# Passing from the per-pixel convolution to the spline convolution: where the first tiles lie, and in which order they are loaded

## The chip, the cores and the metric

The kernel runs on one core of a Trainium2 chip. The core has five engines that work from queues of their own: TensorE (PE in the profile), VectorE (DVE), ScalarE (ACT), GpSimd (POOL) and SyncE (SP). SP issues most transfers here. They are carried out by 16 DMA engines and end by raising a semaphore. The metric is the device time of one execution in microseconds (us), as the median of several runs. Beside it stands one profiled execution, from which all durations come.

## The reference

The input x has 4 images of 16 channels and 256x256 pixels. Two layers follow, each with a residual and with a group norm (8 groups of 2 channels) in front:

```python
x = x + _L0_conv_ref(_gn(x), conv_w, conv_b)
#   out = conv3x3(x): 16*25 numbers a pixel; weights = softmax over the 25
#   result = sum over the 5x5 neighbours of each channel, times weights
x = x + _L1_conv_ref(_gn(x), base_weight, spline_weight, spline_scaler, bias_weight)
#   patches = 3x3 neighbours
#   out = silu(patches) . base_w + B_splines(patches) . spl_w + bias
```

The B-splines are of order 3 on 8 bases: each value of x becomes 8 features, so 16 channels give 128 features, one for each partition of the on-chip memory. The 3x3 sum over them is a matrix product.

## The kernel before, in words

**Layer 0** works in 64 strips: 4 images, 2 halves of 128 rows, 8 strips of 32 columns. A row of the image is a partition. For each 4 columns of a strip, PE makes 400 logits for each pixel from the loaded tiles am and an (L922, L926), ACT takes exp into a tile e (L945), POOL multiplies e by the neighbours u (L950), and DVE sums both halves over the 25 taps into nd (L771). A few steps later each strip is finished: ACT makes the reciprocal's seed from nd (L785, L787), DVE divides and refines (L791, L795, L799), and POOL subtracts the quotient, which stands in nd, from the strip's x (L805). The sum x1 goes to a buffer in the device's memory, x1s. For the last strip of all, POOL issues the two stores itself (L862), behind its L805.

**Layer 1** works in 64 units of 16 image rows (16 units an image). A unit loads its rows of x1 twice: once as 128 features, each channel repeated 8 times (`load_x`, L1029, two transfers of 1 MB into one of three tiles xta, xtb, xtc), and once as plain rows for silu (`load_tiles`, L1041, four transfers of 128 KB into one of three buffers sl). ACT turns the features into distances from the spline's knots (`distance`, L1068), DVE and ACT make the inner part r1 (`inner`, L1077 and L1075), ACT squares it into s1 (`square`, L1082), POOL multiplies to the cube (`cube`, L1089; some squares too, L1085), ACT makes the outer part (`far`, L170), DVE multiplies it and combines both into a ring of rows (`cubed`, `combined`: L173, L176). ACT takes silu of the plain rows (L1051), and PE sums ring and silu over the 3x3 taps (`outputs`, L1229, L1238). Tiles of unit n are those of number n modulo 3 (xt, sl) or modulo 2 (s1).

**The passage.** Layer 1's instructions are placed between those of layer 0's end: while POOL and DVE finish the last strip, ACT already makes unit 0's distance, inner part and square. Each engine runs its queue strictly in order. `in_order` and `behind` fix the order on ACT, DVE, POOL and SP by hand. Three places matter here.

- `load_x(0)`, `load_tiles(0)`, `load_x(1)`, `load_x(2)`, `load_tiles(1)` (L1250 to L1254) set SP's order after layer 0's last loads.
- `start_unit` does unit 0's first steps. Then `first_features` begins with unit 1's distance, which needs xtb, and DVE's inner part of unit 1, which reads it, stands in DVE's queue after the first two chunks of unit 0.
- `for t in sl: sides(t)` (L1268, its memsets are L1257) lets POOL zero the edge columns of the three sl buffers, after the last strip's L805.

**Memory.** Layer 0's pools are given back before layer 1's are made, and layer 1's tiles are laid on the same addresses. `fixed` opens a pool with its tiles, one pool a call, in the order of the calls. The first instruction that touches such a pool's memory waits for the layer-0 instructions that still use it. Of layer 0, in order of address: norm's and transpose's tiles, then an and am (pool im), u and e (one pool, l0), nd, x1's strips xc. Layer 1 before, in order of address: xta, r1a, r1b, s1a, s1b, xtb, pad, ring, xtc, sl (three buffers in one pool), yo. There xtb begins on am and ends on u, xtc lies on e, and the sl pool begins on e and runs over nd.

Of the kernel before, what the change touches and what calls it, by code (L numbers as in the profile page):

```python
# [34 lines left out]
def conv_preact_kernel(  # L35
# [13 lines left out]
    B, C, H, W = x.shape  # L49
    G = 8  # L50
    GC = C // G
    P = 128
# [21 lines left out]
    RT = 2  # L74
    NT = P // (RT * C)
    RD = RT + 2
    RU = 16
# [897 lines left out]
    def layer1(arm, last, marks, seeds):  # L975
# [5 lines left out]
        with ExitStack() as pools:  # L981
            def pool(name, bufs=1, **kw):
                return pools.enter_context(tc.tile_pool(name=f"{name}{arm}", bufs=bufs, **kw))


            def fixed(name, shape, n=1):
                p = pool(name)
                t = [p.tile(shape, F32, name=f"{name}{k}{arm}") for k in range(n)]
                return t

            XT = [P, RU + 1, W]
# [1 line left out]
            SQ = 2 * QR + 2  # L993
            xt0 = fixed("xta", XT)
            r1a, r1b = fixed("r1a", [P, 3 * QR, W])[0], fixed("r1b", [P, QR + 1, W], 2)
            s1s = fixed("s1a", XT) + fixed("s1b", [P, RU, W])
            xt1, pad = fixed("xtb", XT), fixed("pad", [P, W + 2])[0]
            ring = fixed("ring", [P, 2 * RU + 2, W + 2])[0]
            SL = [P, RU // RT, W + 2]
            xtt = xt0 + xt1 + fixed("xtc", XT)  # L1000
            sl = fixed("sl", SL, 3)
            yop = pool("yo", 3)
            ps2 = pool("ps2", 2, space=PSUM)
            py = pool("py", 2, space=PSUM)
# [5 lines left out]
            def rows(t, dims, r):  # L1010

                return bass.AP(tensor=t.tensor, offset=t.offset + r * W, ap=dims)
# [4 lines left out]
            def cuts(u):  # L1017
                lo, hi = span(u)
                return [(a, min(a + QR, hi)) for a in range(lo, hi, QR)]
# [5 lines left out]
            def load_x(n):  # L1025
                b, u = units[n]
                c = cuts(u)
                for a, z in ((c[0][0], c[1][1]), (c[2][0], c[-1][1])):
                    nc.sync.dma_start(  # L1029
                        xs(n, a, z),  # L1030
                        rows(x1s[b], [[CP, 2 * C], [0, SH], [1, (z - a) * W]], u * RU + a),
                    )

            def xs(n, a, z):
                lo = span(units[n][1])[0]
                return xtt[n % 3][:, a - lo : z - lo, :]

            def load_tiles(n):
                b, u = units[n]
                for d in range(RD):  # L1040
                    nc.sync.dma_start(  # L1041
                        sl[n % 3][P // 2 + d : P : RD, :, 1 : W + 1],
                        rows(x1s[b], [[CP, C], [RT * W, RU // RT], [1, W]], u * RU + d),
                    )
# [203 lines left out]
                for b in range(2, B)  # L1248
            ))
            load_x(0)  # L1250
            load_tiles(0)
            load_x(1)
            load_x(2)
            load_tiles(1)  # L1254
            def sides(t):
# [50 lines left out]
    with tc.If(fast > 0) as small_logits:  # L1306
        layer1("", *layer0(False))
    with small_logits.Else():
        layer1("g", *layer0(True))
# [42 lines left out]
```

## Time and profile before

| | |
|---|---|
| median of 3 runs | 2956.73 us (2956.46 to 2959.94) |
| profiled execution, its time | 2963.85 us |
| its span, first to last instruction | 2962.1 us |
| busy: PE, DVE, ACT, POOL | 93%, 96%, 73%, 91% |
| mean granted PE clock | 0.969 of full speed |
| DMA | 647.60 MB, 219 GB/s on the mean |
| layer 0's last matmul begins | 2021.83 us from the span's start |

A row of a timeline has its start, its duration, the engine ("SPq" is the issue of a transfer by SP), the line of the kernel, the operation, the tiles written and read, and how often it was done. Brackets hold the idle time before it and what ended that by the profile. A row of stretches has, for each engine, busy time and number of instructions. A row of waits has who waited for whom, the total in us, how often, and the longest.

### The profile page before, as it was taken

The page shows a single profiled execution, that of the slowest core. Times are in us where ns is not written, and L with a number is a line of the kernel's source. Part 1 is how long each engine was busy: PE and PEld are TensorE (multiplying, and loading weights), DVE is VectorE, ACT ScalarE, POOL GpSimd, SP SyncE. Part 2 cuts the span into 40 slices and gives each one's busy share as a digit, 9 for nine tenths or more (in the row PEclk, how much of TensorE's full clock was granted, in tenths as well). Part 3 has the DMA queues.
Part 4 walks back from the last instruction along what each step waited for, and adds up shares of the span by engine and source line. Part 5 has one row for each costly group of instructions (what it writes and reads, how often), then busy time and mean ns, then how long its engine had stood idle before and what let it go on. Part 6 is the DMA issues. An engine that isn't in the chain of part 4 may idle for free.

```text
span 2962.1 us, 40885 instructions
## 1 busy us (share of the span) xinstructions
PE 2749.8 (93%) x14282; PEld 1490.7 (50%) x14282; DVE 2841.2 (96%) x1866; ACT 2161.9 (73%) x2764; POOL 2703.9 (91%) x1116
## 2 busy tenths in 40 slices
PE   4699999999999999999999989993999999999998
PEld 3466666666666566656656656662323323222222
DVE  7599999999999999999999999996999999999997
ACT  6566876667766567667565554565999999999995
POOL 4399999999999999999999999996898999999895
PEclk7799999999999999999999999996999999999999
DMA  9998999889888789899786766774577676777763
GB/s 276 250 240 230 253 262 249 237 219 253 238 235 231 214 218 239 218 246 243 211 218 173 197 180 173 197 195 155 182 228 221 209 238 208 225 221 223 224 213 102
DMA packets 385736, 647.60 MB, mean 219 GB/s; under 512 B 41842, under 2 KB 250180, under 8 KB 369652
## 3 DMA queue, kind: packets, MB, share of 16 engines
q1 hardware_dynamic: 321556, 609.73, 73.1%
q10 hardware_dynamic: 61920, 31.46, 3.9%
q0 software_dynamic: 2048, 3.72, 0.5%
q8 instruction: 117, 1.92, 0.3%
q14 instruction: 95, 0.78, 0.1%
HBM read 516.18 MB, written 121.15 MB: 215 GB/s over the span
## 4 chain that ended last, share of the span: by engine, by line
DVE 38%; PE 22%; ACT 22%; DMA 7%; issue 6%; SPq 2%; POOL 2%; ACTq 0%; DVEq 0%; POOLq 0%
DVE nd L771 31%; PE lg L922 14%; ACT s L170 4%; PE lg L926 4%; ACT sl L1051 3%; PE yp L1229 3%; ACT xtc L1068 3%; ACT xta L1068 2%; ACT xtb L1068 2%; ACT s1a L1082 2%; ACT s1b L1082 2%; ACT r1b L1075 2%; POOL e L950 2%; DMA am<-hst 2%; DMA an<-hsl 1%
## 5 line engine op out<-in xcount | busy, mean ns | idle before, releaser
L950 POOL TENSOR_TENSOR e<-e,u 128x1600 f32<-128x1600 f32 x512 | 1790.2, 3562 | 54.2 <-ACT e L945 41.5
L922 PE MATMUL lg<-wm,am 128*128 128x400 f32 x4096 | 1737.5, 505 | 73.0 <-ACT e L945 34.2
L771 DVE TENSOR_REDUCE nd<-e 128x128 f32<-128x3200 f32 x512 | 1759.8, 3478 | 34.5 <-POOL e L950 33.9
L926 PE MATMUL lg<-wn,an 97*128 97x400 f32 x2048 | 1345.1, 657 | 15.4 <-DMA an<-hsl 15.2
L945 ACT ACTIVATE e<-lg 128x800 f32<-128x800 f32 x1024 | 834.7, 839 | 583.5 <-PE lg L926 339.0
L922 PEld LDWEIGHTS lg<-wm,am 128*128 128x128 f32 x4096 | 765.2, 193 | 386.1 <-ACT e L945 63.4
L1229 PE MATMUL yp<-ring,wt 128*32 128x512 f32 x6144 | 763.8, 595 | 58.4 <-DVE ring L176 54.4
L926 PEld LDWEIGHTS lg<-wn,an 97*128 97x128 f32 x2048 | 388.5, 190 | 336.9 <-DMA an<-hsl 24.8
L1229 PEld LDWEIGHTS yp<-ring,wt 128*32 128x32 f32 x6144 | 223.1, 109 | 546.2 <-issue 419.9
L1089 POOL TENSOR_TENSOR s1b<-s1b,r1a 128x1024 f32<-128x1024 f32 x96 | 228.9, 2400 | 54.8 <-ACT s1b L1082 54.8
L1089 POOL TENSOR_TENSOR s1a<-s1a,r1a 128x1024 f32<-128x1024 f32 x96 | 228.7, 2400 | 44.3 <-ACT s1a L1082 44.3
L1238 PE MATMUL yp<-sl,ws 128*32 128x512 f32 x1536 | 226.9, 591 | 0.0
L825 ACT ACTIVATE z<-xc,nrm 128x256 f32<-128x256 f32 x240 | 144.0, 600 | 18.2 <-POOL xc L805 14.2
L176 DVE SCALAR_TENSOR_TENSOR ring<-s,s1a 128x1024 f32<-128x1024 f32 x132 | 154.7, 1191 | 0.9
L176 DVE SCALAR_TENSOR_TENSOR ring<-s,s1b 128x1024 f32<-128x1024 f32 (+1 forms) x128 | 151.8, 1206 | 0.3
L1051 ACT ACTIVATE sl<-sl,q 64x2048 f32<-64x2048 f32 (+2 forms) x72 | 136.3, 1903 | 1.7
L1238 PEld LDWEIGHTS yp<-sl,ws 128*32 128x32 f32 x1536 | 65.8, 109 | 113.9 <-issue 109.2
L173 DVE SCALAR_TENSOR_TENSOR s<-xta,cb,s 128x1024 f32<-128x1024 f32 (+2 forms) x90 | 111.1, 1255 | 0.7 <-ACT s L170 0.4
L173 DVE SCALAR_TENSOR_TENSOR s<-xtb,cb,s 128x1024 f32<-128x1024 f32 (+2 forms) x85 | 105.9, 1266 | 0.5 <-ACT s L170 0.4
L173 DVE SCALAR_TENSOR_TENSOR s<-xtc,cb,s 128x1024 f32<-128x1024 f32 (+2 forms) x85 | 105.8, 1266 | 0.4 <-ACT s L170 0.4
L1077 DVE SCALAR_TENSOR_TENSOR r1a<-xtb,cb,pc 128x1024 f32<-128x1024 f32 x63 | 80.0, 1272 | 20.5 <-DMA xtc<-x1s 19.9
L170 ACT ACTIVATE s<-xta,cb 128x1024 f32<-128x1024 f32 (+2 forms) x90 | 96.4, 1084 | 4.4 <-DVE ring L176 4.0
(203 smaller groups left out, 2219.8 us busy)
## 6 DMA issues: line engine op xcount, KB each, us to landing
am<-hst SPq DMA_DIRECT2D x512, 194.6 KB
u<-hs SPq DMA_DIRECT2D x320, 288.0 KB
an<-hsl SPq DMA_DIRECT2D x512, 129.8 KB
xta<-x1s SPq DMA_DIRECT2D x40, 1024.0 KB
xtb<-x1s SPq DMA_DIRECT2D x40, 1024.0 KB
xtc<-x1s SPq DMA_DIRECT2D x40, 1024.0 KB
am<-hst SPq DMA_DIRECT2D x256, 129.8 KB
sl<-x1s SPq DMA_DIRECT2D x256, 128.0 KB
```

Of the source, the lines that this page charges most:

```text
L170: nc.scalar.activation(s, t, AF.Square, scale=-0.5, bias=cb)
L173: nc.vector.scalar_tensor_tensor(p, t, cb2, s, ALU.subtract, ALU.mult)
L176: nc.vector.scalar_tensor_tensor(f, p, 0.0, q, ALU.min, op)
L771: nc.vector.tensor_reduce(nd[:, :, :, j : j + JG].rearrange("p t c j -> p t j c"), e.rearrange("p t j m c d -> p t j c m d"), AX.XY, ALU.add,)
L922: nc.tensor.matmul(lg[:, i, :NL], lhsT=am[:, o : o + P], rhs=wm.rearrange("p m c d -> p (m c d)"), start=True, stop=False,)
L926: nc.tensor.matmul(lg[:, i, :NL], lhsT=an[:, o : o + P], rhs=wn.rearrange("p m c d -> p (m c d)"), start=False, stop=True,)
L945: nc.scalar.activation(ev, lg[:, :, :NL], AF.Exp)
L950: nc.gpsimd.tensor_tensor(e[:, 1].rearrange("p j m c d -> p j (m c) d"), e[:, 0].rearrange("p j m c d -> p j (m c) d"), uv, ALU.mult,)
L1051: nc.scalar.activation(sl[n % 3][0 : P // 2, a:z, 1 : W + 1], sl[n % 3][P // 2 :, a:z, 1 : W + 1], AF.Silu, scale=sc[b][k][P // 2 :], bias ...
L1089: nc.gpsimd.tensor_tensor(s1(n, a, z), s1(n, a, z), r1(n, a, z), ALU.mult)
L1229: nc.tensor.matmul(yp[t * M : (t + 1) * M], lhsT=wt[:, d, e].rearrange("p r o -> p (r o)"), rhs=ring[:, r0 + t * RT + d : r0 + t * RT + d ...
L1238: nc.tensor.matmul(yp[t * M : (t + 1) * M], lhsT=ws[:, e].rearrange("p r o -> p (r o)"), rhs=sl[n % 3][:, t : t + NT + 1 : NT, e : e + W], ...
```

## The change

Two things are edited. The pools of layer 1 are opened in another order, and the three sl buffers get pools of their own: xtb comes right after s1a, then pad, then the first sl buffer (sla), then the ring, and only then s1b, xtc and the two other sl buffers (slb, slc). By address xtb now lies on an and am, pad and sla on am (sla's last 224 bytes on u), s1b and xtc on e, slb on e and nd, slc on nd. And `load_x(1)` stands before `load_tiles(0)`, so SP issues xtb's two transfers ahead of unit 0's silu rows.

```diff
             xt0 = fixed("xta", XT)
             r1a, r1b = fixed("r1a", [P, 3 * QR, W])[0], fixed("r1b", [P, QR + 1, W], 2)
-            s1s = fixed("s1a", XT) + fixed("s1b", [P, RU, W])
+            s1a = fixed("s1a", XT)
             xt1, pad = fixed("xtb", XT), fixed("pad", [P, W + 2])[0]
+            SL = [P, RU // RT, W + 2]
+            sl = fixed("sla", SL)
             ring = fixed("ring", [P, 2 * RU + 2, W + 2])[0]
-            SL = [P, RU // RT, W + 2]
+            s1s = s1a + fixed("s1b", [P, RU, W])
             xtt = xt0 + xt1 + fixed("xtc", XT)
-            sl = fixed("sl", SL, 3)
+            sl += fixed("slb", SL) + fixed("slc", SL)
             yop = pool("yo", 3)
...
             load_x(0)
+            load_x(1)
             load_tiles(0)
-            load_x(1)
             load_x(2)
             load_tiles(1)
```

Lines of the changed kernel behind this place are two higher than before (L1029 is L1031, L1068 is L1070, and so on).

## The prediction

> **What bounds the kernel now.** I read the page's 40 slices first. DVE is busy 96% of the span, PE 93%, POOL 91%, and in the middle of the row only one slice falls for all three: the 28th (1999 to 2073 us; DVE 6 tenths, PE 3, POOL 6), where layer 0 passes to layer 1. So I asked for the stretches there.
>
> ```profile
> 2030.00:2040.00 10.00, 0.00 (x0) 0.00 (x0) 7.67 (x5) 9.30 (x9) 9.79 (x5) 0.50 0.00 0
> 2040.00:2050.00 10.00, 1.89 (x2) 0.18 (x2) 6.63 (x8) 0.00 (x0) 8.78 (x16) 0.50 0.21 70
> 2050.00:2060.00 10.00, 0.00 (x0) 0.00 (x0) 0.00 (x0) 0.00 (x0) 0.00 (x0) 0.50 1.02 330
> 2060.00:2070.00 10.00, 0.00 (x0) 0.00 (x0) 2.98 (x3) 6.31 (x4) 0.00 (x0) 0.50 1.04 364
> ```
>
> The columns are the stretch, then busy time of PE, weight loads, DVE, ACT and POOL, then PE's clock, the DMA share and GB/s. From 2050 to 2060 nobody computes and the DMA engines are full; from 2020 to 2046 it was the other way round: they stand at 0.00. The data comes late because it was asked for late. Next, the timelines of SP, ACT, DVE and PE (start, us, what):
>
> ```profile
> 2004.40 1.24 SPq L1029 DMA_DIRECT2D xta<-x1s  x2
> 2046.15 2.78 SPq L1041 DMA_DIRECT2D sl<-x1s  x4
> 2049.04 3.08 SPq L1029 DMA_DIRECT2D xtb<-x1s  x2
> 2052.16 2.71 SPq L1029 DMA_DIRECT2D xtc<-x1s  x2
> ...
> 2038.85 0.58 ACT L787 ACTIVATE r<-r 128x512 f32<-128x512 f32 x1
> 2063.19 3.80 ACT L1068 ACTIVATE xtb<-xtb,q 128x4096 f32<-128x4096 f32 x1 [23.76 <-DMA xtb<-x1s]
> ...
> 2045.95 1.23 DVE L176 SCALAR_TENSOR_TENSOR ring<-s,s1a 128x1024 f32<-128x1024 f32 x1
> 2067.03 2.47 DVE L1077 SCALAR_TENSOR_TENSOR r1a<-xtb,cb,pc 128x1024 f32<-128x1024 f32 x2 [19.85 <-DMA xtc<-x1s]
> ...
> 2021.83 0.65 PE L926 MATMUL lg<-wn,an 97*128 97x400 f32 x1
> ```
>
> ACT waits 23.76 us for xtb, the second unit's x1. DVE waits 19.85 us for what ACT makes of it: the row names xtc as its releaser, but L1077 reads xtb alone, and ACT's L1068 ends at 2066.99, 0.04 us before DVE starts. And xtb was issued at 2049, behind the silu rows. What held those is in SP's waits:
>
> ```profile
> SPq L1041 <- ACT r L785: 33.2, 1, 33.2
> SPq L1041 <- POOL xc L805: 7.3, 1, 7.3
> ```
>
> SP stands for 40.5 us at the first silu load, until POOL's last L805 (2044.87 for 1.25 us) is done. L785 and L805 are the last to read nd. The three sl buffers are one pool, whose memory runs over layer 0's e and nd; its first load waits for all of that, though buffer 0 itself lies on e.
>
> After the hole the kernel is bound by throughput: from 2300 to 2500 DVE is busy 199.45 of 200 us, ACT 197.53. So a later start of layer 1 moves the end by as much.
>
> **What the skill says.** The Trainium skill, "Perfetto Trace Analysis", section "DMA Instruction — HWDGE (DVE, Sync)": a DMA's row starts when its semaphores are satisfied, ends when the sequencer is free, and holds none of the movement. The trace agrees: issues take 0.55 to 1.6 us, the last x1 stores land 7.2 and 10.7 us after theirs. So 2046.15 is where a wait ended, and what stands behind waits too. "DMA: Bandwidth & Descriptors", section "Issuing engines are not separate DMA queues": all share the same 16 engines, so the last stores (POOL's queue) and SP's loads do compete (share 1.02 above). "SBUF — State Buffer", section "Who interferes with whom": a DMA does not slow a compute engine. Agrees: L173 on 128x1024 takes 1.29 us at 2042.04 with the DMA engines nearly idle and 1.28 us at 2069.41 with them full. "TensorE: Matmul & The Clock Gate", section "What's actually happening": the clock halves after a rest of about 3.4 us and comes back after as much work. The rows show 0.50 during the rest; full clock is back by 2100.
>
> **The change part by part.** I read it in the built instruction order, with waits and addresses.
>
> *xtb ahead of silu's rows.* SP's order becomes xta, xtb, silu 0, xtc, silu 1. xtb now lies on the an and am buffers and waits only for their loads (the DMA engines stand still from 2014 on) and for layer 0's last matmul, which ends at 2022.48. Two issues at 0.62 each, as xta's: out by 2023.8. How long it takes on idle engines no row shows. From above: xtb took 14.1 us from its first issue to ACT's start (2049.04 to 2063.19), with silu rows and stores beside it. From below: 2.10 MB at the 430 GB/s that the stretch 2058 to 2064 reaches is 4.9 us. I take 8, since xta's 2.23 MB were in by about 2012.4 after 2004.40: landed by 2031. Even the upper end gives 2037, before ACT is free at 2039.43. So nothing of it is exposed.
>
> *ACT and DVE.* Their order is unchanged. ACT does L1068 from 2039.45 to 2043.25 instead of 2063.19 to 2066.99. DVE is then held by its own queue: it ends L176 at 2047.18 and goes on at 2047.1 (rows overlap by 0.1) instead of 2067.03. Gain **19.9 us**, not ACT's 23.76: the rest of that is lost, as ACT's next square (2069.53) waits for DVE's two L1077. ACT's L170 for chunks 2 and 3 needs DVE's L176 at 2044.6 and 2047.2, so both are done by 2048.3, before DVE asks at 2049.5.
>
> *Silu's first tile in its own pool.* It lies on am and, for its last 224 bytes, on the u buffer, whose pool also holds e: so it waits for DVE's last L771 (2036.54) instead of L805 (2046.12). Four issues, 2.78 us as before, 2036.6 to 2039.4. Behind it in the queue stand the two of xtc, at most 2.71 us: 2042.1.
>
> *What is late next*, each need being its time before less 19.9. Silu 0: 2052.9 (table load), 13 us after issue. xtc: 2057.2 (L1068 at 2077.09). Silu 1 still waits for L805: issued 2046.4 to 2049.7, needed 2063.0. Then xta's second filling, part one at about 2050, part two when DVE's L173 of chunk 3 is done (2073.34 before, 2053.4 now), needed 2070.6: 17 us, as before. Bytes asked for from 2036.6 on: silu 0.52, xtc 2.10, stores 2.10, silu 0.52, xta 1.05 = 6.3 MB. At 297 GB/s, the lowest of six stretches of 3 us from 2049 to 2067, all of it takes 21.2 us, to 2057.8, and xtc is second in line. If the stores at 2046.7 take half the rate from then on, xtc has 1.0 MB left at most and ends near 2053.5. Four us to spare.
>
> *POOL.* The two memsets of silu 0 move ahead of the last L805: 2 x 0.13 us, so about 0.3 us on L805, the stores and silu 1, which has 13 us. Pad's copy takes new waits, on loads and matmuls done by 2022.5, and runs at 2043.7: nothing. s1b moves onto e's memory: its first square adds a wait for POOL's last L950, over by 2032.4: nothing. Left uncovered, each would cost its 0.3 us or less.
>
> *PE.* It rests from 2022.5 to 2052 instead of 2072, and comes back at half clock either way; it waits for DVE's ring there, so this is not on the path.
>
> Sum: 19.9 us off the profiled execution, span 2962.1 to 2942.2, its time 2963.85 to 2943.95. That execution is 7.1 us above the median of the runs (2956.73), with no reason for the hole to differ, so 2956.73 - 19.9 = **2936.8**.
>
> **The rivals.**
> *xtb late (partial gain).* If xtb in effect started only with silu 0 at 2036.5, or transfers under compute were as slow as in the crowd: 2036.5 + 14.1 = 2050.6, ACT to 2054.4, DVE goes on there: 12.6 us gained, 2944.1. An xtc that lands some us after 2057.2 looks alike, each microsecond costing one. For it: both share engines and SP still stops at silu 0. Against: xtb's wait is the last matmul, and the engines are idle.
> *No change.* The hole stays because xtb is still held by nd's memory. That would leave 2956.7. Against: neither xtb nor silu 0 touches nd now.
> *Slower: PE's clock.* In layer 1 PE is busy 198.27 of 200 us, hardly below DVE. If the shorter rest (30 us instead of 50) left PE with a granted clock below full, PE would set the pace of the 885 us that remain. The gain is gone at 19.9/885, a clock of 0.978; at 0.95 it costs 44 us less 19.9, so 2981. Against: the clock is 1.00 in every stretch from 2100 to 2940, and in layer 0's from 1900 to 2020, without a rest.
>
> **How the numbers follow.** Forecast 0.80, partial 0.11, no change 0.04, slower 0.05. Two medians of one kernel may differ by 3 us (the three runs span 3.5); with the landing times that makes 2931 at the low end. The high end takes in the partial case: 2945. A measurement here can tell about 0.2% (6 us) from nothing; both gaining cases are beyond it, so faster 0.91, same 0.04, slower 0.05.
>
> **What would show it.** xtb's issue at about 2022.5 and silu 0's at 2036.6 on SP; ACT's L1068 on xtb right after L787, at 2039.4, without a wait on DMA; DVE from L176 to L1077 without a gap at 2047; no stretch with all engines at zero. Wrong if ACT waits for xtb or, at about 2057, for xtc; if DVE starts after 2050; or if PE's clock in layer 1 is below 1.00.

## The result, and the profile after

| | before | after |
|---|---|---|
| median of the runs | 2958.34 us (2956.46 to 2960.94, 4 runs) | 2938.64 us (2938.03 to 2940.34, 4 runs) |
| profiled execution, its time | 2963.85 us | 2938.03 us |
| its span | 2962.1 us | 2936.3 us |
| end of DVE's last L771 (below: T) | 2036.54 us | 2030.44 us |
| from T to the end of the span | 925.6 us | 905.9 us |

The ratio of the times is 0.9934, with an interval of 0.9917 to 0.9951: 19.7 us less. The prediction had 2936.8, and 19.9 us less. Three of the four runs before are the ones it started from; the fourth lifts their median by 1.6 us.

The spans differ by more, 25.8 us. About 6.1 us of that lie ahead of the passage: DVE's last reduction of layer 0 ends at 2030.44 instead of 2036.54, and nothing in layer 0 was edited. The same changed kernel, profiled again, had it at 2034.46. So every time below that is to be compared is counted from T, the end of DVE's last L771 in its own execution. From T on the changed kernel is 19.7 us shorter in the profile too.

Two of the changed kernel's SP waits carry most of the explanation. First SP's timeline, then the view of its waits, both of the kernel after:

```profile
2016.40 1.16 SPq L1031 DMA_DIRECT2D xtb<-x1s  x2
2030.47 2.51 SPq L1043 DMA_DIRECT2D sla<-x1s  x4
2033.02 1.25 SPq L1031 DMA_DIRECT2D xtc<-x1s  x2
2040.15 2.73 SPq L1043 DMA_DIRECT2D slb<-x1s  x4
```

```profile
SPq L1031 <- PE lg L926: 15.0, 1, 15.0
SPq L1043 <- DVE nd L799: 13.5, 1, 13.5
SPq L1043 <- POOL xc L805: 5.8, 1, 5.8
```

SP now stands for the last matmul and sends xtb 14.0 us before T; before, it was 12.5 us after T. Then it stands 13.5 us at the first silu row. The row names L799, but that instruction runs from 2030.32 to 2031.03, and silu's issue starts before its end, at 2030.47, 0.03 us behind the end of L771. So it is the last L771 that is waited for, as the prediction had it. Only the second silu tile still waits for L805.

What ACT and DVE make of that, in the timelines of the kernel after:

```profile
2032.75 0.58 ACT L787 ACTIVATE r<-r 128x512 f32<-128x512 f32 x1
2033.24 3.79 ACT L1070 ACTIVATE xtb<-xtb,q 128x4096 f32<-128x4096 f32 x1
...
2026.92 3.52 DVE L771 TENSOR_REDUCE nd<-e 128x128 f32<-128x3200 f32 x1
2030.32 0.71 DVE L799 TENSOR_TENSOR nd<-nd,r 128x512 f32<-128x512 f32 x1
2039.86 1.23 DVE L176 SCALAR_TENSOR_TENSOR ring<-s,s1a 128x1024 f32<-128x1024 f32 x1
2041.00 2.46 DVE L1079 SCALAR_TENSOR_TENSOR r1a<-xtb,cb,pc 128x1024 f32<-128x1024 f32 x2
...
2050.57 0.21 DVE L189 TENSOR_REDUCE sums<-st 128x16 f32<-128x64 f32 x1
2055.00 1.28 DVE L1079 SCALAR_TENSOR_TENSOR r1a<-xtc,cb,pc 128x1024 f32<-128x1024 f32 x1 [4.22 <-issue]
```

ACT takes xtb right behind L787, with no wait. From the start of DVE's L176 to its first L1079 on xtb there are 1.14 us; before, there were 21.08 (2045.95 to 2067.03). The difference is 19.94 us. From that L1079 on to the end, layer 1 takes 895.3 us, as against 895.07. A gap of 4.22 us remains, ahead of the first instruction on xtc. The experiments come back to it.

The stretches of the passage, kernel after, with the columns as in the prediction:

```profile
2020.00:2030.00 10.00, 0.00 (x0) 0.00 (x0) 10.00 (x4) 9.81 (x9) 10.00 (x4) 0.51 0.34 144
2030.00:2040.00 10.00, 0.00 (x0) 0.00 (x0) 7.12 (x10) 8.12 (x7) 9.65 (x12) 0.50 0.72 256
2040.00:2050.00 10.00, 5.22 (x14) 0.77 (x18) 9.78 (x9) 7.53 (x7) 7.22 (x9) 0.50 0.84 252
2050.00:2060.00 10.00, 10.00 (x92) 3.28 (x88) 5.67 (x8) 9.92 (x7) 7.83 (x5) 0.95 0.83 280
2100.00:2922.00 822.00, 815.75 (x7260) 251.76 (x7256) 810.64 (x746) 797.65 (x546) 735.66 (x376) 1.00 0.67 214
```

No stretch has the compute engines at zero any more, and the DMA engines, which stood still from 2020 to 2046 before, work under the compute. PE rests, comes back at half clock, and is granted 1.00 from 2100 to 2922.

### The profile page after: what moved, and what is told of

Read it like the earlier page. It is cut to its first block, busy times and chain, and to the rows that moved or that the text cites. A ratio compares the mean times of both kernels' runs of the same rounds, so it can differ in the third digit from the quotient of the medians.

```text
span 2936.3 us, 40887 instructions
## 1 busy us (share of the span) xinstructions
PE 2742.2 (93%) x14282; PEld 1486.3 (51%) x14282; DVE 2840.3 (97%) x1866; ACT 2161.5 (74%) x2764; POOL 2703.7 (92%) x1116
## 4 chain that ended last, share of the span: by engine, by line
DVE 39%; ACT 21%; PE 20%; DMA 8%; issue 7%; POOL 3%; SPq 2%; ACTq 0%; DVEq 0%; POOLq 0%
DVE nd L771 32%; PE lg L922 12%; ACT s L170 4%; PE lg L926 3%; PE yp L1231 3%; ACT xtc L1070 2%; ACT xtb L1070 2%; ACT xta L1070 2%; POOL e L950 2%; ACT s1a L1084 2%; DMA an<-hsl 2%; ACT s1b L1084 2%; ACT r1b L1077 1%; DMA am<-hst 1%; DVE ring L176 1%
## 5 line engine op out<-in xcount | busy, mean ns | idle before, releaser
L771 DVE TENSOR_REDUCE nd<-e 128x128 f32<-128x3200 f32 x512 | 1762.9, 3494 | 30.3 <-POOL e L950 29.9
L176 DVE SCALAR_TENSOR_TENSOR ring<-s,s1a 128x1024 f32<-128x1024 f32 x132 | 158.7, 1233 | 0.9
L176 DVE SCALAR_TENSOR_TENSOR ring<-s,s1b 128x1024 f32<-128x1024 f32 (+1 forms) x128 | 155.6, 1246 | 0.3
L785 ACT ACTIVATE r<-nd 128x512 f32<-128x512 f32 x64 | 38.3, 598 | 78.9 <-DVE nd L799 78.9
L170 ACT ACTIVATE s<-xtc,cb 128x1024 f32<-128x1024 f32 (+2 forms) x85 | 91.8, 1094 | 1.3 <-DVE ring L176 0.7
L170 ACT ACTIVATE s<-xtb,cb 128x1024 f32<-128x1024 f32 (+2 forms) x85 | 91.8, 1093 | 0.8 <-DVE ring L176 0.4
L1079 DVE SCALAR_TENSOR_TENSOR r1a<-xtc,cb,pc 128x1024 f32<-128x1024 f32 x63 | 82.7, 1312 | 4.5 <-issue 4.5
```

The costliest lines, as they stand in the source:

```text
L170: nc.scalar.activation(s, t, AF.Square, scale=-0.5, bias=cb)
L176: nc.vector.scalar_tensor_tensor(f, p, 0.0, q, ALU.min, op)
L771: nc.vector.tensor_reduce(nd[:, :, :, j : j + JG].rearrange("p t c j -> p t j c"), e.rearrange("p t j m c d -> p t j c m d"), AX.XY, ALU.add,)
```

## The experiments

Each kernel was profiled once, and timed side by side with the kernel before. T is given in us from the span's start. The columns "on xtb", "on xtc" and "on xta" are DVE's first inner-part instruction on unit 1, 2 and 3, in us after that execution's T; the last column is the end of the span after T.

| kernel | median of runs (range, runs) | ratio to before | T | on xtb | on xtc | on xta | end |
|---|---|---|---|---|---|---|---|
| before | 2958.34 (2956.46 to 2960.94, 4) | 1 | 2036.54 | 30.5 | 44.4 | 60.7 | 925.6 |
| after | 2938.64 (2938.03 to 2940.34, 4) | 0.9934 [0.9917, 0.9951] | 2030.44 | 10.6 | 24.6 | 40.8 | 905.9 |
| order only | 2945.58 (2939.59 to 2949.3, 4) | 0.995 [0.9933, 0.9967] | 2034.19 | 12.3 | 32.4 | 48.7 | 913.3 |
| pools only | 2943.59 (2939.6 to 2947.57, 4) | 0.9954 [0.9938, 0.9971] | 2028.02 | 14.9 | 28.9 | 45.2 | 909.8 |
| own pools, old places | 2942.23 (2940.74 to 2948.13, 4) | 0.9951 [0.9934, 0.9968] | 2029.92 | 15.0 | 28.9 | 45.2 | 909.9 |
| xtb last | 2958.78 (2957.68 to 2968.2, 12) | 1.0008 [0.9998, 1.0017] | 2030.73 | 30.5 | 44.6 | 60.8 | 925.6 |
| after, again | 2941.78 (2939.99 to 2942.06, 5) | 0.994 [0.9926, 0.9953] | 2034.46 | 10.6 | 24.6 | 40.8 | 905.4 |
| silu early | 2941.24 (2939.71 to 2945.86, 5) | 0.9941 [0.9927, 0.9954] | 2035.06 | 10.6 | 23.7 | 40.0 | 904.7 |
| silu and xtc early | 2934.99 (2929.92 to 2940.55, 5) | 0.9917 [0.9903, 0.9932] | 2032.99 | 10.6 | 20.3 | 37.0 | 901.7 |
| the same, sla off u | 2935.76 (2933.9 to 2939.01, 5) | 0.9923 [0.991, 0.9937] | 2031.96 | 10.6 | 20.3 | 37.0 | 901.6 |

The kernel before had a median of 2957.79 us (15 runs) beside the four kernels from "order only" to "xtb last", and of 2960.05 us (9 runs) beside the last four, which ran on another chip. The runs of one kernel scatter by some us, so differences of a few us are read from the columns after T.

### The order alone

The kernel before, with its pools, and xtb ahead of the silu rows:

```diff
             load_x(0)
-            load_tiles(0)
             load_x(1)
+            load_tiles(0)
             load_x(2)
```

> The kernel before with xtb's two loads ahead of silu's rows and nothing else. In this layout xtb's end lies on u, so its first load waits for DVE's last L771 (call its end T). Theory (the order is what counts, the place only sets which end of layer 0 it waits for): issue at T + 0.1, landed 7 us later as in the changed kernel, ACT 3.8 us, so DVE goes on at about T + 12 instead of T + 10.6. Silu 0 still waits for L805 (T + 9.7) and xtc stands behind it and beside the stores, so some more is lost there: 1.5 to 4 us behind the changed kernel, 16 to 18.5 us ahead of the one before, about 2940 us. Rival (the new places are what counts): xtb is held as long as before, the hole stays, 2957 us.

Measured: DVE goes on at T + 12.3, as worked out, but the end lies 7.4 us behind the changed kernel's (913.3 against 905.9). SP, DVE and ACT in the timeline of this kernel:

```profile
2030.71 3.48 DVE L771 TENSOR_REDUCE nd<-e 128x128 f32<-128x3200 f32 x1
2034.22 1.16 SPq L1029 DMA_DIRECT2D xtb<-x1s  x2
2043.81 2.62 SPq L1041 DMA_DIRECT2D sl<-x1s  x4
2046.47 3.31 SPq L1029 DMA_DIRECT2D xtc<-x1s  x2
2046.47 2.47 DVE L1077 SCALAR_TENSOR_TENSOR r1a<-xtb,cb,pc 128x1024 f32<-128x1024 f32 x2 [1.63 <-ACT xtb L1068]
2055.00 1.28 ACT L1051 ACT_TABLE_LOAD   x1 [2.71 <-DMA sl<-x1s]
2062.73 3.81 ACT L1068 ACTIVATE xtc<-xtc,q 128x4096 f32<-128x4096 f32 x1 [3.42 <-DMA xtc<-x1s]
2066.63 1.28 DVE L1077 SCALAR_TENSOR_TENSOR r1a<-xtc,cb,pc 128x1024 f32<-128x1024 f32 x1 [10.36 <-ACT xtc L1068]
```

At its old place xtb ends on the u buffer, so it waits for the last L771 (issue at T + 0.03) rather than for the last matmul. The silu rows still wait for L805, until T + 9.6, and now it is xtc that stands behind them. The hole is not gone, it has moved one unit on: 10.36 us ahead of DVE's first instruction on xtc, where the changed kernel has 4.22. The 6.1 us between the two are ACT's waits for silu's rows (2.71 us) and then for xtc (3.42 us), neither of which the changed kernel has. The expectation named both transfers, but with 1.5 to 4 us behind the changed kernel it made their cost too small.

### The pools alone

The changed kernel's pools and places, and the old order:

```diff
             load_x(0)
-            load_x(1)
             load_tiles(0)
+            load_x(1)
             load_x(2)
```

> The changed kernel with the old order of loads: silu 0, then xtb. Theory: SP now stands at silu 0 only until T (end of the last L771) instead of L805 at T + 9.7. Its four issues take 2.5 us, xtb follows at T + 2.7 to T + 3.9 and lands at T + 10 to T + 11.5, ACT needs 3.8 us more: DVE goes on at T + 13.5 to T + 15. That is 3 to 4.5 us behind the changed kernel, about 2942 us. Rival (the order is needed, pools alone give nothing): the hole stays, 2957 us.

The timeline of this kernel:

```profile
2028.04 2.51 SPq L1043 DMA_DIRECT2D sla<-x1s  x4
2030.59 1.25 SPq L1031 DMA_DIRECT2D xtb<-x1s  x2
2039.08 3.80 ACT L1070 ACTIVATE xtb<-xtb,q 128x4096 f32<-128x4096 f32 x1 [8.17 <-DMA xtb<-x1s]
2042.91 2.47 DVE L1079 SCALAR_TENSOR_TENSOR r1a<-xtb,cb,pc 128x1024 f32<-128x1024 f32 x2 [4.25 <-ACT xtb L1070]
```

Silu's issue ends its wait 0.02 us after T (2028.02), and xtb goes out 2.5 us behind it. ACT waits 8.17 us for it instead of 23.76, and DVE goes on at T + 14.9, as expected. The end is 15.8 us earlier than before, 3.9 us later than after.

### Pools of their own, places as before

Do the new places matter, or only that one pool became three? The kernel before, with one line changed:

```diff
-            sl = fixed("sl", SL, 3)
+            sl = fixed("sla", SL) + fixed("slb", SL) + fixed("slc", SL)
```

Every tile keeps its address.

> The kernel before with the three sl buffers in pools of their own at the old addresses; order of the loads and all other places as before. Theory: the first buffer lies on e alone, so its load waits for the last L771 and not for the last reader of nd; from there everything is as in the changed pools with the old order: about 2942 us, within 1 us of that kernel. Rival (xtb's and sla's new places have a worth of their own): more than 2 us slower than that kernel. Second rival (the pool is not what joins the waits): the hole stays, 2957 us.

Its timeline:

```profile
2026.44 3.48 DVE L771 TENSOR_REDUCE nd<-e 128x128 f32<-128x3200 f32 x1
2029.94 2.51 SPq L1041 DMA_DIRECT2D sla<-x1s  x4
2032.56 1.21 SPq L1029 DMA_DIRECT2D xtb<-x1s  x2
2041.05 3.80 ACT L1068 ACTIVATE xtb<-xtb,q 128x4096 f32<-128x4096 f32 x1 [8.24 <-DMA xtb<-x1s]
2044.89 2.47 DVE L1077 SCALAR_TENSOR_TENSOR r1a<-xtb,cb,pc 128x1024 f32<-128x1024 f32 x2 [4.33 <-ACT xtb L1068]
```

It is the kernel with the new places over again, step by step and to 0.1 us at the end. With the same addresses, the first silu load now starts 0.02 us after the last L771, where in the kernel before it waited for L805, 9.6 us after T. So the wait for nd came with the pool and not with the buffer's own bytes, and one line is worth 15.7 of the 19.7 us. With the old order the new places are worth nothing, because silu's tile stands ahead of xtb and waits for L771 in either place. What they are worth with the new order was not run. In the kernel with the order alone, xtb at its old place brings DVE on 1.7 us later than in the changed kernel (T + 12.28 against T + 10.56), from which some 1.7 us are an estimate of it.

### xtb last

The changed kernel, with both silu tiles ahead of xtb:

```diff
             load_x(0)
-            load_x(1)
             load_tiles(0)
-            load_x(2)
             load_tiles(1)
+            load_x(1)
+            load_x(2)
```

> The changed kernel's pools and places, but xtb and xtc loaded behind silu 0 and silu 1, whose load waits for L805. Theory (a wait at the head of SP's queue makes the hole, wherever the tiles lie): xtb is issued at about T + 12.5 as before, beside the stores; DVE goes on at T + 27 to T + 31 and the time is 2954 to 2958 us. Rival (the places make the gain): 2938 to 2942 us.

Its timeline:

```profile
2030.76 2.51 SPq L1043 DMA_DIRECT2D sla<-x1s  x4
2040.41 2.55 SPq L1043 DMA_DIRECT2D slb<-x1s  x4
2043.01 3.29 SPq L1031 DMA_DIRECT2D xtb<-x1s  x2
2057.43 3.80 ACT L1070 ACTIVATE xtb<-xtb,q 128x4096 f32<-128x4096 f32 x1 [23.81 <-DMA xtb<-x1s]
2061.27 2.47 DVE L1079 SCALAR_TENSOR_TENSOR r1a<-xtb,cb,pc 128x1024 f32<-128x1024 f32 x2 [19.90 <-DMA xtc<-x1s]
```

The hole is back whole, with all pools and places as in the changed kernel: ACT's wait of 23.81 us, DVE's of 19.90, the end at T + 925.6, a ratio of 1.0008 (the median, 2958.78, lies just above the 2954 to 2958 expected). What stands at the head of SP's queue, and how long, makes the hole. xtb's memory has been free since the last matmul and nobody profits.

### What is left: the gap ahead of xtc

ACT's timeline in the changed kernel, ahead of DVE's first instruction on xtc:

```profile
2048.19 2.37 ACT L1053 ACTIVATE sla<-sla,q 64x256 f32<-64x256 f32 x2
2050.58 0.64 ACT L1084 ACTIVATE s1b<-r1a 128x512 f32<-128x512 f32 x1
2051.12 3.79 ACT L1070 ACTIVATE xtc<-xtc,q 128x4096 f32<-128x4096 f32 x1
```

DVE ends L189 at 2050.78 and then stands for 4.22 us. Its row names no releaser ("issue"), but ACT's distance of unit 2, L1070 on xtc, starts at 2051.12 and ends at 2054.91, 0.09 us before DVE goes on. xtc had long landed by then, as ACT does not wait for it. ACT is simply at other work: silu of unit 0 (2046.89 to 2050.56 with the table load ahead of it) and unit 1's small square stand ahead of it. Two places for silu and the distance were tried, with the changed kernel run again beside them.

> The changed kernel once more, to stand beside the next three. Theory: 2938 to 2940 us; layer 1 from DVE's first L1079 to the end takes 895 us as in the kernel before.

It repeats the steps after T to 0.02 us, and the end to 0.5 us; layer 1 takes 894.9 us from DVE's first L1079. Its median, 2941.78, lies above the 2938 to 2940 expected; that of the kernel before is 1.7 us higher in this series, too.

**Silu early.** ACT has a rest after unit 1's distance, where silu of unit 0 fits:

```diff
                 distance(1, *span(units[1][1]))
+                silu(0)
                 for c in range(2):
...
                 ps.append(far(0, 4))
-                silu(0)
                 next(pre)
```

> The changed kernel with silu of unit 0 right behind unit 1's distance, in ACT's idle time, instead of behind chunk 4's outer part. What the passage still costs is DVE's gap of 4.2 us before its first work on xtc. Theory A (the gap is ACT's length: table load and silu, 3.65 us, stand on the path): 3 to 4 us faster than the changed kernel. Theory B (ACT's small square of unit 1, which stands ahead of xtc's distance and waits for DVE's third L1079, sets the gap): ACT then idles in front of that square, and only about 1 us is gained.

The timelines of ACT and DVE in this kernel:

```profile
2041.67 1.28 ACT L1053 ACT_TABLE_LOAD   x1
2042.96 2.36 ACT L1053 ACTIVATE sla<-sla,q 64x256 f32<-64x256 f32 x2
...
2053.06 1.27 DVE L1079 SCALAR_TENSOR_TENSOR r1a<-xtb,cb,pc 128x1024 f32<-128x1024 f32 x1
2054.37 0.63 ACT L1084 ACTIVATE s1b<-r1a 128x512 f32<-128x512 f32 x1 [2.94 <-DVE r1a L1079]
2054.90 3.79 ACT L1070 ACTIVATE xtc<-xtc,q 128x4096 f32<-128x4096 f32 x1
2058.78 1.28 DVE L1079 SCALAR_TENSOR_TENSOR r1a<-xtc,cb,pc 128x1024 f32<-128x1024 f32 x1 [3.39 <-issue]
```

Silu is done early, at no cost, but the distance gains only 0.8 us. ACT's queue now stops at unit 1's small square (L1084 on 128x512), which waits 2.94 us for DVE's third inner part on xtb. In the changed kernel silu had filled that very wait and ended 0.84 us behind it (2050.56, where that inner part ends at 2049.72): no more was to be had. The median of the runs is not told apart from the changed kernel's.

**Silu and xtc early.** So the distance has to pass the small square as well:

```diff
                 combined(0, 4, ps[4])
-                next(pre)
                 distance(2, *span(units[2][1]))
+                next(pre)
```

> Silu of unit 0 early as in the run before, and xtc's distance ahead of unit 1's small square. xtc has landed long before. Theory: ACT ends xtc's distance at about the time that DVE is through with chunk 4, the gap of 4.2 us closes, DVE is busy from there on: 3.5 to 4.5 us faster than the changed kernel, about 2934.5 us. Rival (POOL or the silu rows of unit 1, which land late beside the stores, set the pace next): less than 2 us.

Its timelines:

```profile
2049.30 3.79 ACT L1070 ACTIVATE xtc<-xtc,q 128x4096 f32<-128x4096 f32 x1
2053.12 0.21 DVE L189 TENSOR_REDUCE sums<-st 128x16 f32<-128x64 f32 x1
2053.24 1.27 DVE L1079 SCALAR_TENSOR_TENSOR r1a<-xtc,cb,pc 128x1024 f32<-128x1024 f32 x1
```

The gap is gone: DVE starts on xtc at T + 20.25 instead of T + 24.56, and the end comes at T + 901.7 instead of 905.4 to 905.9. That is 3.7 to 4.2 us, the size of the gap. The median in the same series is 2934.99 against 2941.78. That is more than the gap, within a scatter of 5 us to either side, and the two intervals of the ratio overlap a little, so the size is taken from the profile. This version is ahead of both kernels.

**The same, and sla off u.** The 224 bytes with which sla lies on the u buffer hold its load until T. Opened ahead of pad, sla keeps clear of u:

```diff
-            xt1, pad = fixed("xtb", XT), fixed("pad", [P, W + 2])[0]
+            xt1 = fixed("xtb", XT)
             SL = [P, RU // RT, W + 2]
             sl = fixed("sla", SL)
+            pad = fixed("pad", [P, W + 2])[0]
```

> As the run before, with sla ahead of pad, so that sla no longer touches u. Theory: sla's load waits for the last matmul alone and is issued right behind xtb, some 13 us earlier; nobody waits for it, so the time is that of the run before within 1 us. Rival (sla's landing is what ACT waits for once silu is early): 1 us or more faster than the run before.

SP's timeline in this kernel, whose T is 2031.96:

```profile
2017.92 1.16 SPq L1032 DMA_DIRECT2D xtb<-x1s  x2
2019.13 2.74 SPq L1044 DMA_DIRECT2D sla<-x1s  x4
2031.99 1.21 SPq L1032 DMA_DIRECT2D xtc<-x1s  x2
```

The silu rows go out 12.8 us before T, right behind xtb, so those 224 bytes did hold them for 13 us. The time stays (901.6 against 901.7): xtc lies on e and waits for L771 anyway, and silu's rows have slack in both. A wait of 13 us at the head of the queue is worth nothing if what stands behind it is not late.

## Why the prediction was right, step by step

**The cause.** It named the pool of the three silu buffers, which runs over nd, and xtb behind it in SP's queue. Both are shown: the pool by the kernel that changes nothing else (15.7 us), the queue by the kernel that puts xtb last (the hole whole again). Of the rivals, xtb late and no change both fell: ACT has no wait for xtb, and xtb is held by the last matmul alone. The two halves do not add up, and the prediction did not part them: the order alone brings 12.3 us, the pools alone 15.8, both 19.7. Each alone removes part of the same chain of waits.

**The gain.** 19.9 us were read off as DVE's gap and not ACT's wait of 23.76; measured, 19.94 at DVE, and 19.7 at the end and in the runs. The 0.2 us between them are layer 1, which takes 895.3 us instead of 895.07. The predicted times have to be set back by 6.1 us, as that execution's T came earlier. Then xtb's issue (2022.5 less 6.1) is due at 2016.4 and came at 2016.40; sla's (2036.6) is due at 2030.5 and came at 2030.47; L1070 on xtb (2039.45) is due at 2033.35 and came at 2033.24; DVE's first L1079 (2047.1) is due at 2041.0 and came at 2041.00; silu 1's issue (2046.4) is due at 2040.3 and came at 2040.15. That an issue begins where its wait ends, as the Trainium skill has it ("Perfetto Trace Analysis", section "DMA Instruction — HWDGE (DVE, Sync)"), is what made SP's three numbers workable; all five came within 0.15 us. The 0.3 us put on POOL's last L805 were 0.1: it ends at T + 9.69 instead of T + 9.58. What the prediction set beside that section was the landing of the last stores, which POOL issues. For SP's loads the trace shows it at xtb: the row of its issue ends at 2017.56, and its bytes move until about 2023.5.

**xtb's landing.** Eight us were taken, between 4.9 and 14.1. The stretches of the kernel after show the bytes moved 6 to 8 us behind the first issue at 2016.40:

```profile
2022.00:2024.00 2.00, 0.00 (x0) 0.00 (x0) 2.00 (x2) 1.97 (x3) 2.00 (x2) 0.50 0.69 287
2024.00:2026.00 2.00, 0.00 (x0) 0.00 (x0) 2.00 (x1) 1.97 (x2) 2.00 (x1) 0.50 0.00 0
```

The share of 0.69 in the one and 0.00 in the next puts it near 2023.5, so about 7 us. ACT asks 9.7 us after that, and nothing is exposed.

**xtc.** Its need was put at 2057.2, so at 2051.1 here; ACT's L1070 on it starts at 2051.12. The "four us to spare" came from a worst case, in which xtc has 1.0 MB left when the last stores take half the rate. That does not follow from the prediction's own rate: counted from 2036.6, 297 GB/s bring the 2.62 MB of sla and xtc in 8.8 us, by 2045.4, ahead of the stores at 2046.7. Here SP issued sla and xtc from 2030.47 to 2034.27. The stretch from 2030 to 2040 moves 2.56 MB (256 GB/s), so by this estimate they were in by about 2040.5, when POOL had only begun to issue the stores (2040.43), and some ten us were spare. The step stood; its size was off on the safe side.

**PE.** The slower rival wanted a clock below 0.978 in layer 1. The clock is 0.50 in the rest, 0.95 from 2050 to 2060, 0.90 and 0.93 in the next two stretches, behind waits of PE between 2062 and 2068, and 1.00 from 2080 on; layer 1 took 895.3 us from DVE's first L1079. This is also what the Trainium skill says ("TensorE: Matmul & The Clock Gate", section "What's actually happening"): the clock goes down in a rest and comes back with work. Here PE's last matmul of layer 0 ends at 2016.37, and the clock is 1.00 from 2018 to 2020 and 0.55 from 2020 to 2022. PE works without a break from 2048.59, and the clock is 0.77 from 2050 to 2052 and 1.00 from 2052 to 2054. The shorter rest left no lower clock behind.

**What it did not see.** DVE's gap ahead of xtc (4.22 us) was part of "layer 1, unchanged". It was, and the last experiments show that some 4 us could be had there, by ACT's order and not by SP's.

## What to carry to other kernels

Where a stretch has all engines at zero and the DMA engines full, look at the instruction that holds the head of the issuing queue, ask which memory it waits for, and whether its own buffer lies there or only another buffer of the same pool; a pool for each buffer can remove the wait without moving a byte. Count the gain at the engine that sets the pace, and then follow each transfer behind the moved one: here the order alone only handed the hole on to the next tile. When an instruction is pulled ahead in a strict queue, look at what it used to cover: silu early gained 0.8 us until the instruction it had hidden was passed as well.

## What was not expected

The end of layer 0 (T) lay between 2028.02 and 2036.54 us over the profiled executions, with nothing edited ahead of it and with 2030.44 and 2034.46 for one and the same kernel. That is more than most of the edits here move, and its cause stays open. Counted from T, the same steps repeat to about 0.1 us (DVE's first instruction on xtb at 10.55 or 10.56 in the changed kernel, in its repetition and in the last three kernels). A row's releaser can also be the wrong one: DVE's 19.90 us with xtb last are put down to xtc's transfer, while the instruction reads xtb alone and starts 0.04 us behind the end of ACT's L1070.
